# Two-layer transformer kernel: the order of scores, divisions, rotary work and layer norm in the attention stages of its first attention layer

## The chip, the core and the metric

The kernel runs on one core of a Trainium2 chip. Its engines are TensorE (PE in the profile, with weight loads as PEld), VectorE (DVE), ScalarE (ACT), GpSimd (POOL) and SyncE (SP, which here only issues DMAs). Each engine works through its own queue in order. The metric is the device time of one execution in microseconds. Three runs before the change took 939.63, 939.76 and 940.93 us; the median is 939.76.

## The reference

The input is x of shape (8, 512, 256) in float32. All matmuls but the quantised one are float32. There are two layers, each x + attention(norm(x)) + feed-forward(norm(x)).

```python
xn = _layernorm(x)
# layer 0 (the code's first attention): 16 heads of 64, rotary positions, causal softmax
q = rope(xn @ Wq + bq); k = rope(xn @ Wk + bk); v = xn @ Wv + bv
attn = softmax(where(causal, q @ k.T / 8, -1e9))
x = x + (attn @ v) @ Wo + bo + quantised_linear(xn)
xn = _layernorm(x)
# layer 1: a gated comparison as attention, and a mix over time as feed-forward
c = (xn @ left) @ (xn @ right).T / 16
x = x + ((c > threshold) * softmax(c + bias)) @ xn + time_mix(xn)
```

The rotary step multiplies each pair of halves by cosines and sines and adds: h = l * cos + swapped(l) * sin. The change touches the first attention alone (the one with 16 heads).

## The kernel before, in words

The first attention is cut into 16 stages, numbered `at` 0 to 15: 8 sequences by 2 groups of 8 heads. The order of instructions on every engine is that of the program text (`manual_schedule`); nothing is rearranged. Inside a stage the work is this.

- **Projections.** `project_qk` (matmuls at L400) makes the queries (`which` 0) or keys (`which` 1) of four heads: 8 matmul records into two PSUM banks, which ScalarE moves to a tile `l` with the bias (L405). Four DMAs on SP's queue copy `l` with its halves exchanged into `y`. `turn_qk` is the rotary step: two products on VectorE (L417, one for `h`, one for `y`), and their sum on GpSimd (L432). `l` and `y` have two buffers each. `project_v` (L443) makes the values, in two halves of two banks; ScalarE copies them out (L449), they go to DRAM, and `load_v` brings them back in the layout that the weighting needs.
- **Scores.** The 16 blocks of 32 query rows, called i, are causal: block i has 32(i+1) columns. `UNITS` packs them into nine units of two PSUM banks each, (15), (14, 0), (13, 1) and so on to (8, 6) and (7). `RUNS` groups the units: runs 0 to 3 have two units each, run 4 has unit (7) alone. `scores(at, run)` is TensorE's part (L480).
- **Softmax.** `soften(at, run)` reads each bank once on VectorE (L508: mask, minimum of the negated scores, and the copy to a tile `p`), which frees the bank, and takes the exponential with its sum on ScalarE (L512). `divide` takes reciprocals on VectorE (L523) and divides on GpSimd (L531), or, with `on_act`, on ScalarE (L529) for the last unit of the run. `turn` transposes 32x32 blocks on VectorE (L551) into the tiles `t0` to `t3`. The `p` tiles have four buffers, so unit 11 takes the buffer of unit 15 once that has been transposed.
- **Weighting and output.** `weigh(at)` (L568) multiplies the values with the transposed chances into four banks; `keep_weighed` moves them out on ScalarE (L582). `output_product` (L362) applies Wo, `add_output` adds on VectorE (L371).
- **Layer norm of later sequences.** `look_at` takes the statistics on VectorE, `prepare` applies them (L171) and takes the greatest magnitude (L301); `transpose_x` turns the result on TensorE (L318). In stages 12 and 13 some work of the quantised layer joins: `round_input` on GpSimd (L190), `clip` on VectorE (L196, L197).

PSUM has one pool of eight banks:

```python
ps = ctx.enter_context(tc.tile_pool(name="ps", bufs=8, space=PSUM))
```

Banks are handed out in turn: a new bank is the one that was handed out eight banks earlier, and the first matmul into it waits until that one's reader has finished. In stage `at` of the kernel before, TensorE's order is: run 0 of the scores (4 banks), the weighting of stage at-1 (4), run 1 (4), the queries of stage at+1 (4), run 2 (4), the values of stage at+1 (4), in even stages the transposes of the next sequence (2), runs 3 and 4 (6), the output product of stage at-1 (2), the keys of stage at+2 (4). Stage 15 and what follows it are written out by hand.

## Time and profile before

| | |
|---|---|
| median of three runs | 939.76 us |
| profiled execution | 939.1 us |
| its span, first to last instruction | 937.2 us |
| granted clock of TensorE | 0.999 |
| TensorE busy | 923.8 us (99%) |
| VectorE busy | 787.4 us (84%) |
| GpSimd busy | 540.0 us (58%) |
| ScalarE busy | 533.0 us (57%) |

Busy times are of the engines' own instructions; issuing DMAs and waiting on semaphores doesn't count. A line of a timeline gives the start and the length in us, engine, source line, operation, the tiles as output<-input, their shapes, and how many instructions were merged into the line; a bracket at its end gives the idle time before it and what ended it. Lengths of neighbouring lines overlap a little, so sums go from start to start. The slices cut the span into 40 equal parts, each digit the busy share in tenths.

### The profile page before, as it was taken

The page shows a single profiled execution, that of the slowest core. Times are in us where ns is not written, and L with a number is a line of the kernel's source. Part 1 is how long each engine was busy: PE and PEld are TensorE (multiplying, and loading weights), DVE is VectorE, ACT ScalarE, POOL GpSimd, SP SyncE. Part 2 cuts the span into 40 slices and gives each one's busy share as a digit, 9 for nine tenths or more (in the row PEclk, how much of TensorE's full clock was granted, in tenths as well). Part 3 has the DMA queues.
Part 4 walks back from the last instruction along what each step waited for, and adds up shares of the span by engine and source line. Part 5 has one row for each costly group of instructions (what it writes and reads, how often), then busy time and mean ns, then how long its engine had stood idle before and what let it go on. Part 6 is the DMA issues. An engine that isn't in the chain of part 4 may idle for free.

```text
span 937.2 us, 27414 instructions
## 1 busy us (share of the span) xinstructions
PE 923.8 (99%) x10491; PEld 600.8 (64%) x10491; DVE 787.4 (84%) x2431; ACT 533.0 (57%) x1488; POOL 540.0 (58%) x688
## 2 busy tenths in 40 slices
PE   9998999999999999999999999999999999999998
PEld 5446565656666575757565656666657777777776
DVE  4998889898799889978997899899899588888854
ACT  3585555656575656474747566555667434445553
POOL 2676765655665757566665756678666424444311
PEclk9999999999999999999999999999999999999999
DMA  7667453525443545263535435453444132211011
GB/s 212 193 166 201 112 128 126 122 80 138 146 105 96 133 136 131 75 159 92 136 91 160 108 98 137 136 145 106 103 114 126 47 101 79 76 57 39 23 34 34
DMA packets 60930, 105.40 MB, mean 112 GB/s; under 512 B 7552, under 2 KB 38272, under 8 KB 60800
## 3 DMA queue, kind: packets, MB, share of 16 engines
q1 hardware_dynamic: 58928, 102.01, 40.1%
q10 hardware_dynamic: 1872, 1.64, 0.7%
q8 instruction: 83, 1.36, 0.6%
q14 instruction: 47, 0.39, 0.1%
HBM read 39.14 MB, written 28.84 MB: 73 GB/s over the span
## 4 chain that ended last, share of the span: by engine, by line
PE 92%; DVE 4%; issue 1%; ACT 1%; POOL 1%; SPq 0%; DMA 0%; DVEq 0%; ACTq 0%; POOLq 0%
PE pq L400 22%; PE av L568 14%; PE sc L480 13%; PE pw L362 12%; PE pv L443 10%; PE po L727 5%; PE pg L689 3%; PE pvv L701 3%; PE pk L674 3%; PE trc L714 1%; PE plr L240 1%; PE c L646 1%; DVE t L551 1%; PE acc L205 1%; DVE p L508 1%
## 5 line engine op out<-in xcount | busy, mean ns | idle before, releaser
L512 ACT ACTIVATE p<-p,nm 128x64 f32<-128x64 f32 (+15 forms) x512 | 259.9, 512 | 123.1 <-DVE nm L508 98.3
L531 POOL TENSOR_SCALAR p<-p,rs 128x512 f32<-128x512 f32 (+4 forms) x504 | 263.3, 543 | 44.0 <-DVE rs L523 41.9
L432 POOL TENSOR_TENSOR h<-h,y 128x1024 f32<-128x1024 f32 x62 | 161.0, 2596 | 188.9 <-DVE y L417 106.6
L508 DVE CUSTOM_DVE_ANT_0 p<-sc,cmask 128x64 f32<-128x64 f32 (+15 forms) x512 | 190.3, 434 | 61.5 <-PE sc L480 61.5
L551 DVE STREAM_TRANSPOSE t<-p 128x256 f32<-128x256 f32 (+3 forms) x640 | 192.1, 366 | 18.2 <-POOL p L531 18.1
L480 PE MATMUL sc<-h,h 64*32 64x416 f32 (+15 forms) x4096 | 138.7, 393 | 1.9 <-POOL h L432 1.2
L568 PE MATMUL av<-t,vr 32*64 32x192 f32 (+15 forms) x4096 | 128.8, 392 | 4.0 <-issue 4.0
L568 PEld LDWEIGHTS av<-t,vr 32*64 32x64 f32 x4096 | 123.2, 131 | 9.1 <-issue 7.8
L480 PEld LDWEIGHTS sc<-h,h 64*32 64x32 f32 x4096 | 78.8, 106 | 76.0 <-issue 56.5
L405 ACT ACTIVATE l<-pq,cs 128x512 f32<-128x512 f32 x128 | 84.7, 683 | 66.8 <-PE pq L400 54.4
L417 DVE TENSOR_TENSOR y<-y,cs 128x1024 f32<-128x1024 f32 x64 | 110.7, 1729 | 5.8 <-DMA y<-l 5.3
L362 PE MATMUL pw<-wo,att 128*128 128x256 f32 x512 | 114.8, 382 | 0.0
L400 PE MATMUL pq<-xnT,wq 128*128 128x512 f32 x256 | 114.6, 599 | 0.2 <-ACT xnT L321 0.2
L443 PE MATMUL pv<-wv,xnT 128*128 128x512 f32 x256 | 114.3, 599 | 0.0
L400 PE MATMUL pq<-xnT,wk 128*128 128x512 f32 x256 | 112.9, 593 | 0.6 <-DVE nm L508 0.6
L362 PEld LDWEIGHTS pw<-wo,att 128*128 128x128 f32 x512 | 95.9, 190 | 18.5 <-issue 6.1
L512 ACT ACTIVATION_READ_ACCUMULATOR p<-p,nm 128x1 f32 x512 | 97.3, 190 | 0.0
L400 PEld LDWEIGHTS pq<-xnT,wk 128*128 128x128 f32 x256 | 48.6, 190 | 56.6 <-issue 54.1
L443 PEld LDWEIGHTS pv<-wv,xnT 128*128 128x128 f32 x256 | 47.3, 190 | 57.9 <-issue 54.1
L417 DVE TENSOR_TENSOR h<-l,cs 128x1024 f32<-128x1024 f32 x64 | 79.5, 1243 | 4.5 <-ACT l L405 4.5
L400 PEld LDWEIGHTS pq<-xnT,wq 128*128 128x128 f32 x256 | 47.2, 190 | 56.0 <-issue 48.8
L582 ACT ACTIVATE att<-av,cs 128x512 f32<-128x512 f32 x64 | 38.7, 688 | 71.4 <-PE av L568 71.4
(113 smaller groups left out, 949.8 us busy)
## 6 DMA issues: line engine op xcount, KB each, us to landing
y<-l SPq DMA_DIRECT2D x256, 128.0 KB, 2.3
va<-v SPq DMA_DIRECT2D x32, 512.0 KB, 3.1
vr<-va SPq DMA_DIRECT2D x64, 256.0 KB, 4.8
x<-in_x SPq DMA_DIRECT2D x15, 512.0 KB, 4.2
xnf<-xnT SPq DMA_DIRECT2D x8, 512.0 KB, 3.3
x1f<-x SPq DMA_DIRECT2D x7, 512.0 KB, 2.7
out<-y SPq DMA_DIRECT2D x14, 256.0 KB, 2.2
cut_wo<-xnf SPq DMA_DIRECT2D x5, 512.0 KB, 4.2
```

Source lines behind the costliest of these rows:

```text
L362: nc.tensor.matmul(pw[:, j, :], atts[at, p][:, tok], wo[:, 4 * (at % NH) + p, :], start=(p == 0), stop=(p == 3),)
L400: nc.tensor.matmul(pb, w[:, g, k, bass.ts(t, P)], xnT[b][:, k, :], start=(k == 0), stop=(k == NK - 1),)
L405: nc.scalar.activation(l[:, t, :], pb, AF.Identity, bias=cs[:, bias : bias + 1])
L417: nc.vector.tensor_tensor(dst, src, table[:, None, :].to_broadcast([P, 2, S]), ALU.mult)
L432: (engine or nc.gpsimd).tensor_tensor(h, h, y, ALU.add)
L443: nc.tensor.matmul(pb.rearrange("p (g n) -> p g n", g=2), xnT[b][:, k, bass.ts(2 * half + j, P)], wqkv[2][:, 2 * g : 2 * g + 2, k, :], sta ...
L480: nc.tensor.matmul(scored[at, i][e][j * Q : j * Q + Q, :], q[rows, j % 2, bass.ts(i, Q)], k[rows, j % 2, :n], start=True, stop=True,)
L508: nc.vector.tensor_tensor_reduce(p[:, e, col : col + n], sc, cmask[:, S - n :], -1.0 / L**0.5, BIG, ALU.add, ALU.min, nm[:, c : c + 1],)
L512: nc.scalar.activation(p[:, e, col : col + n], p[:, e, col : col + n], AF.Exp, bias=nm[:, c : c + 1], scale=-1.0, accum_out=sm[:, c : c + 1],)
L531: nc.gpsimd.tensor_scalar(p, p, rs[:, c : c + 1], 1.0, ALU.mult, ALU.mult)
L551: nc.vector.transpose(turned[at][c][:, :, at_ : at_ + (n - 1) * pitch(c) + 1 : pitch(c), :], p[:, :, c * P : c * P + n * Q].rearrange("p e ...
L568: nc.tensor.matmul(banks[j][e * L : e * L + L, i * Q :], vs[at][rows, m, c, bass.ts(e, L)], t[c][rows, e, m * pitch(c) + m : m * pitch(c) ...
```

## The change

Stage 1 is written out as it was (with its last transposes of `turn(1, 4)` at its end, where they stood at the start of stage 2). In stages 2 to 14 the order changes:

- The scores come in two stretches: runs 0 and 1 together after the weighting, and runs 2, 3 and 4 together between the two halves of the values.
- The weighting of stage at-1 opens the stage. Beside it stand the rotary step of the second queries of this stage (`turn_qk(2 * at + 1, 0)`, which was in the stage before), the statistics of a later sequence and, in most even stages, its layer norm.
- On GpSimd the sum of the second queries, which stood between the divisions of runs 2 and 3, is gone from there, so that the divisions of runs 2, 3 and 4 follow each other. The divisions of run 0 keep their place ahead of the sum of the second keys, and those of run 1 ahead of the sum of the first queries; what moves is VectorE's part: the eviction of run 1 now comes before run 0's reciprocals and products, and that of run 2 only after both rotary steps and both transposes.
- The divisions of unit (8, 6) go from GpSimd to ScalarE (`on_act`).
- Run 4 is transposed at the end of its own stage. `turn` can now take one unit of a run (`part`).

In the hand-written part, run 2 of stage 14 moves there from the loop. The number of instructions is the same on TensorE, VectorE and SP's DMA issues; ScalarE gets 48 divisions that GpSimd had.

```diff
@@ -536,14 +536,14 @@
         def pitch(c):
             return NT * 4 - 4 * c - 1
 
-        def turn(at, run):
+        def turn(at, run, part=slice(None)):
 
             if at not in turned:
                 turned[at] = [
                     prob.tile([P, 2, 4 * pitch(c) + 1, Q], F32, tag=f"t{c}", name=f"t_{at}_{c}", bufs=1)
                     for c in range(NT)
                 ]
-            for i in (i for us in RUNS[run] for i in us):
+            for i in (i for us in RUNS[run][part] for i in us):
                 p = chances.pop((at, i))
                 for c in range(i // 4 + 1):
                     n = min(4, i + 1 - 4 * c)
@@ -810,87 +810,127 @@
         x_next.append(load_x(2))
         turn(0, 3)
         project(2, 1)
-        for at in range(1, last):
+
+        at = 1
+        scores(1, 0)
+        turn(0, 4)
+        soften(1, 0)
+        weigh(0)
+        keep_weighed(0)
+        load_rest()
+        load_second()
+        fetch(0)
+        turn_qk(4, 1)
+        load_v(1)
+        divide(1, 0)
+        turn_qk(5, 1)
+        scores(1, 1)
+        soften(1, 1)
+        turn(1, 0)
+        divide(1, 1)
+        project(2, 0)
+        scores(1, 2)
+        soften(1, 2)
+        turn_qk(4, 0)
+        turn(1, 1)
+        divide(1, 2)
+        nc.gpsimd.tensor_tensor(bob, bob, rw[:, 2, :], ALU.add)
+        add_biases(0)
+        project_v(2)
+        scores(1, 3)
+        soften(1, 3)
+        turn_qk(5, 0)
+        turn(1, 2)
+        divide(1, 3)
+        scores(1, 4)
+        soften(1, 4)
+        finish(0)
+        turn(1, 3)
+        project(3, 1)
+        divide(1, 4)
+        turn(1, 4)
+        for at in range(2, last):
             b, g = divmod(at, NH)
             two = at + 2 <= last
+            clips = at in (last - 3, last - 2)
             if g == 0 and b < B - 1:
                 fetch(b)
-            scores(at, 0)
-            turn(at - 1, 4)
-            soften(at, 0)
             if at == last - 3:
                 scale_of_x()
             weigh(at - 1)
+            if at > 2:
+                turn_qk(2 * at + 1, 0)
+            if at == 2 or g == 1 and 1 <= b < B - 2:
+                look_at(b + 1 + g)
+            turn_qk(2 * at + 2, 1)
+            if g == 0 and 1 < b < B - 2:
+                prepare(b + 1)
             keep_weighed(at - 1)
-            if at == 1:
-                load_rest()
-                load_second()
-                fetch(0)
-            turn_qk(2 * at + 2, 1)
             load_v(at)
-            if at in (last - 3, last - 2):
+            if clips:
                 s_ = at - last + 3
                 fetch_output(s_, output_tile(f"x1e_{s_}"))
                 xnl = fetch_input(s_, work.tile([P, NK, S], F32, tag="xnl", name=f"xnl_{s_}"))
+            if at == last - 2:
+                first_norm = norm(0, xpool.tile([P, NT, D], F32, tag="x", name="yn_0"))
+            scores(at, 0)
+            scores(at, 1)
+            soften(at, 0)
+            project_qk(2 * at + 2, 0)
+            soften(at, 1)
             divide(at, 0)
             turn_qk(2 * at + 3, 1)
-            if at == last - 2:
-                first_norm = norm(0, xpool.tile([P, NT, D], F32, tag="x", name="yn_0"))
-            scores(at, 1)
-            soften(at, 1)
-            turn(at, 0)
             if at == 2:
-                look_at(2)
+                prepare(2)
             elif at == 4:
                 spread_rest()
                 spread_second()
-            elif g == 1 and 1 <= b < B - 2:
-                look_at(b + 2)
+            elif at == last - 1:
+                first_norm()
+            project_qk(2 * at + 3, 0)
+            if clips:
+                round_input(xnl)
+            turn(at, 0)
             divide(at, 1)
-            if at == last - 1:
-                first_norm()
-            project(at + 1, 0)
-            if at in (last - 3, last - 2):
-                round_input(xnl)
-            scores(at, 2)
-            soften(at, 2)
             turn_qk(2 * at + 2, 0)
             turn(at, 1)
-            if at in (last - 3, last - 2):
+            if at == last - 4:
+                prepare(b + 2)
+            if clips:
                 xq = work.tile([P, NK, S], BF16, tag="xq", name=f"xq_{s_}")
                 clip(xnl, xq)
-            divide(at, 2)
-            if at == 2:
-                prepare(2)
-            elif g == 1 and 1 <= b < B - 2:
-                prepare(b + 2)
             if at == last - 1:
                 turn_qk(2 * at + 3, 0)
-            if at == 1:
-                nc.gpsimd.tensor_tensor(bob, bob, rw[:, 2, :], ALU.add)
-                add_biases(0)
-            project_v(at + 1)
-            if at == last - 1:
+                project_v(at + 1)
                 break
+            project_v(at + 1, (0,))
+            for run in (2, 3, 4):
+                scores(at, run)
+            soften(at, 2)
+            soften(at, 3)
+            project_v(at + 1, (1,))
             if g == 0 and b < B - 1:
                 transpose_x(b + 1)
                 if b + 2 < B:
                     x_next.append(load_x(b + 2))
-            scores(at, 3)
-            soften(at, 3)
-            turn_qk(2 * at + 3, 0)
-            turn(at, 2)
-            divide(at, 3)
-            scores(at, 4)
+            divide(at, 2)
+            turn(at, 2, slice(0, 1))
+            divide(at, 3, on_act=True)
+            turn(at, 2, slice(1, 2))
             soften(at, 4)
-            if at in (last - 3, last - 2):
+            if clips:
                 for half in range(2):
                     add_quantised(s_, half, xq, line(f"u_{s_}_{half}"))
-            finish(at - 1)
-            turn(at, 3)
+            for half in range(2):
+                output_product(at - 1, half)
+            turn(at, 3, slice(0, 1))
+            divide(at, 4)
+            turn(at, 3, slice(1, 2))
+            for half in range(2):
+                add_output(at - 1, half)
+            turn(at, 4)
             if two:
                 project(at + 2, 1)
-            divide(at, 4)
             if g == 0 and b < B - 1:
                 add_biases(b)
             if at == last - 4:
@@ -898,9 +938,11 @@
 
 
         at = last
-        scores(at - 1, 3)
-        soften(at - 1, 3)
+        for run in (2, 3):
+            scores(at - 1, run)
+            soften(at - 1, run)
         nc.sync.dma_start(w2, second.rearrange("j (k p) n -> p j k n", p=P))
+        divide(at - 1, 2)
         turn(at - 1, 2)
         divide(at - 1, 3)
         scores(at - 1, 4)
```

## The prediction

> **What bounds the kernel now.** I read the page's busy shares and slices first, then TensorE's timeline for one stage, then its waits, then the timelines of VectorE and GpSimd over the same stretch.

> ```profile
> PE 923.8 (99%) x10491; PEld 600.8 (64%) x10491; DVE 787.4 (84%) x2431; ACT 533.0 (57%) x1488; POOL 540.0 (58%) x688
> PE   9998999999999999999999999999999999999998
> DVE  4998889898799889978997899899899588888854
> PEclk9999999999999999999999999999999999999999
> ```

> TensorE has work all the time, at the full granted clock; VectorE is second. The profiled execution took 939.1 us, 0.7 below the median of 939.76, with a span of 937.2. TensorE idles 13.4 us in all, so no order of the same matmuls can gain more than that.

> TensorE's timeline, one stage (stage 5):

> ```profile
> 254.71 1.95 PE L480 MATMUL sc<-h,h 64*32 64x512 f32 x48
> 256.59 8.02 PE L568 MATMUL av<-t,vr 32*64 32x512 f32 x256
> 264.54 2.12 PE L480 MATMUL sc<-h,h 64*32 64x448 f32 x64
> 266.58 7.13 PE L400 MATMUL pq<-xnT,wq 128*128 128x512 f32 x16
> 273.65 2.01 PE L480 MATMUL sc<-h,h 64*32 64x384 f32 x64
> 275.59 7.13 PE L443 MATMUL pv<-wv,xnT 128*128 128x512 f32 x16
> 282.65 2.39 PE L480 MATMUL sc<-h,h 64*32 64x320 f32 x80
> 284.97 7.17 PE L362 MATMUL pw<-wo,att 128*128 128x256 f32 x32
> 291.98 7.03 PE L400 MATMUL pq<-xnT,wk 128*128 128x512 f32 x16
> 298.94 1.95 PE L480 MATMUL sc<-h,h 64*32 64x512 f32 x48
> ```

> Start to start the pieces take: run 0 of the scores 1.88, weighting 7.95, run 1 2.05, queries 7.06, run 2 1.94, values 7.06, runs 3 and 4 2.32, output 7.01, keys 6.96; 44.23 in all, without a gap. Between any two groups of score banks lie some 7 us of other matmuls: the time VectorE has to empty the banks.

> TensorE's waits in stages 2 to 13 come to 3.2 us (line L480 adds 1.2 in stage 14).

> VectorE (rotary products L417) and GpSimd (rotary sums L432, divisions L531), from their timelines around 305 and 103 us:

> ```profile
> 303.96 1.22 DVE L417 TENSOR_TENSOR y<-y,cs 128x1024 f32<-128x1024 f32 x1
> 305.25 1.20 DVE L417 TENSOR_TENSOR h<-l,cs 128x1024 f32<-128x1024 f32 x1
> 306.36 3.38 DVE L417 TENSOR_TENSOR y<-y,cs 128x1024 f32<-128x1024 f32 x1
> ...
> 305.32 3.34 POOL L432 TENSOR_TENSOR h<-h,y 128x1024 f32<-128x1024 f32 x1 [5.80 <-DVE rs L523]
> 312.74 2.37 POOL L432 TENSOR_TENSOR h<-h,y 128x1024 f32<-128x1024 f32 x1
> ...
> 101.29 5.67 POOL L531 TENSOR_SCALAR p<-p,rs 128x384 f32<-128x384 f32 x8 [0.46 <-DVE rs L523]
> 237.76 3.65 POOL L531 TENSOR_SCALAR p<-p,rs 128x384 f32<-128x384 f32 x8 [0.47 <-DVE rs L523]
> ```

> A product that meets a sum takes 3.38 instead of 1.22 and ends when the sum has ended and 1.1 us more have passed; the sum takes 3.34 instead of 2.37. The eight divisions that met two products at 103.9 to 106.4 took 5.67 instead of 3.65. So a product and a GpSimd instruction take turns. Transposes and the scores' eviction show no such loss beside divisions.

> **The change, part by part.** TensorE's matmuls are the same ones. What changes is how much of them lies between a bank's filling and its next use. In stages 2 to 13 the new order is weighting, runs 0 and 1 (eight banks at one go), queries, half the values, runs 2, 3, 4 (ten banks), the other half of the values, output, keys. The eight PSUM banks go round, so run 4 takes the banks of unit 11, the first of run 2, and waits in TensorE's queue until VectorE has evicted it (L508). Behind that wait stands everything else of TensorE. And VectorE now does two rounds of rotary products and both transposes of runs 0 and 1 ahead of that eviction.

> I take time 0 as the start of the eviction of unit 15, 0.22 after its matmuls end (317.88+0.97 to 319.07 in the trace). TensorE then needs: unit 14, 0.94; run 1, 2.05; queries 7.06; half the values 3.5; run 2, 1.94; run 3, 0.8 of 2.32 = 1.86; less 0.22. It wants run 4's bank at 17.1.

> VectorE and GpSimd, each step as soon as its engine and its input are there:
> - eviction of runs 0 and 1: 2.58 + 2.76 (rows at 300.25 and 309.98) = 5.34; reciprocals to 5.5. ScalarE's exponentials of run 0 start at about 1.4, behind the four weighted banks (2.42), take 3.4 and are in time.
> - two products (key, second half), 1.14 each start to start: to 7.8. GpSimd's divisions of run 0 meet them and take turns; unit 15's two divisions (0.65 each) end at 9.1, the rest of run 0 (1.3 + 0.6) at 11.0.
> - transposes of run 0 from 9.1: 2.7, to 11.8; reciprocals to 12.0.
> - GpSimd's rotary sum 11.0 to 13.4. VectorE's next two products (the first queries) want to start at 12.0, wait to 13.4, end at 15.65.
> - only then run 1's divisions: 3.65, to 19.3; transposes follow, ending at 20.0.
> - eviction of unit 11: 1.38, to 21.4.

> TensorE stands from 17.1 to 21.5: 4.4. Run 4 takes 0.47 to 22.0; the second half of the values wants unit 10's banks, free at 22.6: 0.6 more. **5.0 us per stage.** From there: values 3.5, output 7.0, keys 6.96 to 40.1. VectorE and its suppliers: eviction of runs 2 and 3 to 25.5; exponentials of run 3, 3.95 on ScalarE, to 28.6; transposes of unit 10 to 30.4; run 4's eviction 31.1; ScalarE's four divisions (rows 534 and 474 ns) about 2 us, then run 4's exponentials to 33.8; its divisions 35.0; transposes of unit 8, two output additions (1.2) and run 4's transposes to 37.6. The weighting, which now has no run 0 ahead as cover (1.88), finds its input 2.5 us early.

> The other parts:
> - The second queries' rotary work moves beside the weighting: four products and two sums, taking turns, some 6.5 us, plus 3.3 for a layer norm in the even stages, with 9.1 us and the 2.5 in hand: no cost. If that cover were gone, scores of run 0 would wait for the sum.
> - The four exchange copies per projection stay in SP's order. The keys' last copy waits for the second queries' sum, now a stage later, with the next load of values queued behind it; the copy lands in 2.3, the load in 4.8, and both are wanted tens of us later: nothing.
> - Fewer changes of tile shape on TensorE: run 2's 1.94 against run 1's 2.05 bounds this at 0.1 gained or lost per stage, taken at nothing.
> - Stage 2: weighting without cover costs 1.9 more (it already waited 0.86 at 118.84). Its layer norm (3.2) falls where VectorE waits for GpSimd anyway: 0.6.
> - Stage 11: layer norm of the last sequence ahead of run 2's eviction, four of 0.5 and one of 1.22: 3.15.
> - Stages 12 and 13: rounding on GpSimd (1.12) ahead of run 1's divisions and clipping (1.1) ahead of run 2: 2.2 each, 4.4.
> - Stage 14: 3.5 us more of values on TensorE, against two more products held up by a sum: wait 4.8.
> - Old gaps that close as TensorE is late: 2.7.

> Sum: 12 x 5.0 + 1.9 + 0.6 + 3.15 + 4.4 + 4.8 - 2.7 = 72. From 939.1 that is 1011; with the 0.7 to the median, **1012**.

> A rule on the clock, weighed: the trace's clock stays at 1.00 in its windows through its longest gap, 2.31 us (L568, at 72.6), and no row shows a longer one once the work has begun. [...] I keep the full clock, as the nearest rows show it.

> **The rivals.**
> - Products and GpSimd don't take turns there, or find free places. Then unit 15's divisions end at 6.9, run 0's transposes at 10.6, products at 13.1, run 1's transposes at about 16, unit 11 at 17.4: 0.3 + 0.6 per stage. 12 x 0.9 + 1.9 + 0.6 + 3.15 + 4.4 + 1.5 - 2.7 = 20, so 959. Against it: 5.67 for 3.65, 3.38 for 1.22. Chance 0.12.
> - Not slower: VectorE reaches unit 11's eviction by 17.1 in each stage. That decides it; it needs 4.3 us less between 0 and 21.4, when VectorE's own instructions there add up to 17.3 without any wait. Then the 4.4 of gaps in stages 2 to 14 go: 935 to 941. Only evictions much shorter than the rows would give it. Chance 0.05.
> - The end of the stage is late too: ScalarE carries four more divisions and the values' evictions ahead of run 4's exponentials. Up to 2.5 us later costs nothing; beyond that every us costs 12. At 4.5 late: 24, 1036. Against it: ScalarE was 57% busy. Chance 0.08.
> - The clock falls after each wait: if the 3.5 us of values that follow took half as long again, 13 x 1.75 = 23, 1035. For it: waits longer than any shown; against: clock 1.00 so far. Chance 0.08.

> **How the numbers follow.** My own case has 0.67, and its own range is 980 to 1025: a wait of 2.5 to 6 per stage. The range that should hold the time 8 times in 10 reaches down into the case without turns and up to the two late ones: 958 to 1034. A change of under 0.2% (1.9 us) can't be told from none. Faster 0.03, same 0.02 (both from the second rival), slower 0.95.

> **What would show it.** Among TensorE's waits a new row for L480, released by VectorE's nm L508, about 12 to 13 times, 4 to 5 us each; a smaller one of L443 behind it. Stages of 49 us. VectorE's products before run 0's and run 1's transposes lengthened, and VectorE waiting for L531. No wait of L568 beyond stage 2. Wrong would be: run 4 following run 3 without a gap, or the wait at another line; a lower granted clock would point to the last rival.

## The result and the profile after

| | before | after |
|---|---|---|
| median, us | 940.35 (939.63 to 941.96, 4 runs) | 1034.47 (1034.33 to 1036.46, 4 runs) |
| span of the profiled execution, us | 937.2 | 1034.6 |
| TensorE busy, us | 923.8 | 955.1 |
| TensorE idle, us | 13.4 | 79.5 |
| mean granted clock of TensorE | 0.999 | 0.949 |

The change makes the kernel 10% slower: the ratio is 1.1007, with a 95% interval of 1.0989 to 1.1024. The prediction was 1012, with a range of 958 to 1034. Of the 97.4 us between the two spans, 66.1 are idle time of TensorE and 31.3 are the same 10491 matmul records taking longer. Idle time was forecast (72); the longer matmuls were a rival's (23).

From the page of the kernel after, the busy times, and the slices of TensorE, VectorE and the granted clock:

```profile
PE 955.1 (92%) x10491; PEld 610.6 (59%) x10491; DVE 808.3 (78%) x2431; ACT 547.1 (53%) x1536; POOL 544.6 (53%) x640
...
PE   9989979898989898989898969698897999999998
...
DVE  4997696889687868786888696787869948888864
...
PEclk9999999999989898989898989899898999999999
```

From the twelfth slice to the 26th every second digit of TensorE falls, and the clock's digit falls with it in each of them. All in all the clock says that some 105 us (0.051 of 1034.6, doubled since it falls to a half, 0.50 in the window from 306 to 308 below) were spent at half clock.

TensorE's waits, largest first (line, releaser; us in total, times, longest):

```profile
PE sc L480 <- DVE nm L508: 66.6, 13, 9.8
PE av L568 <- issue: 4.9, 2, 2.6
```

One wait, 13 times, at the line and by the releaser that the prediction named. TensorE's timeline for stage 5, which answers to the one shown of before:

```profile
276.77 7.88 PE L568 MATMUL av<-t,vr 32*64 32x512 f32 x256
284.58 3.98 PE L480 MATMUL sc<-h,h 64*32 64x512 f32 x112
288.49 7.13 PE L400 MATMUL pq<-xnT,wq 128*128 128x512 f32 x16
295.46 3.60 PE L443 MATMUL pv<-wv,xnT 128*128 128x512 f32 x8
298.99 3.74 PE L480 MATMUL sc<-h,h 64*32 64x384 f32 x128
306.68 1.31 PE L480 MATMUL sc<-h,h 64*32 64x256 f32 x16 [3.96 <-DVE nm L508]
308.02 5.53 PE L443 MATMUL pv<-wv,xnT 128*128 128x512 f32 x8
313.40 7.07 PE L362 MATMUL pw<-wo,att 128*128 128x256 f32 x32
320.30 7.03 PE L400 MATMUL pq<-xnT,wk 128*128 128x512 f32 x16
```

The next weighting starts at 327.26, so the stage takes 50.49 where it took 44.23. Start to start, the piece from run 2 to the end of run 4 takes 9.03 (298.99 to 308.02) against 1.94 + 2.32 = 4.26: 4.77 more. The values take 3.53 + 5.38 against 7.06: 1.85 more. All else together is 0.36 less. The two halves of the values have the same shape and count; the half ahead of the wait takes 3.60, the half behind it 5.53.

The clock over that stretch, by windows (busy time and count of TensorE, weight loads, VectorE, ScalarE and GpSimd, then the granted clock, DMA share, GB/s):

```profile
302.00:304.00 2.00, 0.73 (x32) 0.26 (x12) 1.58 (x6) 0.00 (x0) 2.00 (x6) 1.00 0.47 132
304.00:306.00 2.00, 0.00 (x0) 0.00 (x0) 2.00 (x8) 0.06 (x1) 2.00 (x3) 0.74 0.54 188
306.00:308.00 2.00, 1.31 (x16) 0.43 (x17) 2.00 (x13) 2.00 (x9) 0.83 (x1) 0.50 0.00 0
308.00:314.00 6.00, 5.98 (x11) 2.92 (x12) 4.56 (x26) 6.00 (x26) 2.93 (x7) 0.68 0.00 0
314.00:320.00 6.00, 6.00 (x29) 5.28 (x29) 5.61 (x22) 3.46 (x10) 3.46 (x8) 1.00 0.28 90
```

0.74 over two us means half clock for 1.04 of them, so it fell at 304.96, in the midst of the gap; 0.68 over six means half clock for 3.84, so it came back at 311.8. In between lie run 4 and most of the second half of the values.

VectorE and GpSimd in the same stage, with lines left out; time 0 of the prediction, the start of unit 15's eviction, is 285.76:

```profile
292.38 1.22 DVE L417 TENSOR_TENSOR y<-y,cs 128x1024 f32<-128x1024 f32 x1
294.78 2.79 DVE L551 STREAM_TRANSPOSE t<-p 128x256 f32<-128x256 f32 x9 [1.18 <-POOL p L531]
...
297.61 2.35 DVE L417 TENSOR_TENSOR h<-l,cs 128x1024 f32<-128x1024 f32 x1
299.87 1.21 DVE L417 TENSOR_TENSOR y<-y,cs 128x1024 f32<-128x1024 f32 x1
302.16 1.49 DVE L551 STREAM_TRANSPOSE t<-p 128x256 f32<-128x256 f32 x5 [1.07 <-POOL p L531]
303.90 1.48 DVE L551 STREAM_TRANSPOSE t<-p 128x256 f32<-128x256 f32 x5 [0.26 <-POOL p L531]
305.31 0.52 DVE L508 CUSTOM_DVE_ANT_0 p<-sc,cmask 128x384 f32<-128x384 f32 x1
```

```profile
291.38 5.18 POOL L531 TENSOR_SCALAR p<-p,rs 128x512 f32<-128x512 f32 x6 [9.27 <-DVE rs L523]
296.52 2.35 POOL L432 TENSOR_TENSOR h<-h,y 128x1024 f32<-128x1024 f32 x1
298.85 5.66 POOL L531 TENSOR_SCALAR p<-p,rs 128x448 f32<-128x448 f32 x8
```

VectorE's product of 297.61 lasts 2.35 instead of 1.2 because GpSimd's sum runs from 296.52 to 298.87; the eight divisions behind it take 5.66 instead of 3.65 because they share the time with that product's second half and the next one. VectorE waits 1.18, 1.07 and 0.26 for divisions. That is the chain that holds unit 11's eviction (305.31) back.

In the last stages the same wait is longer. TensorE in stages 11 to 13, then what VectorE waited for in stage 12:

```profile
617.44 1.32 PE L480 MATMUL sc<-h,h 64*32 64x256 f32 x16 [7.77 <-DVE nm L508]
...
673.80 1.31 PE L480 MATMUL sc<-h,h 64*32 64x256 f32 x16 [9.79 <-DVE nm L508]
...
728.99 1.31 PE L480 MATMUL sc<-h,h 64*32 64x256 f32 x16 [7.51 <-DVE nm L508]
```

```profile
664.63 1.65 DVE L417 TENSOR_TENSOR y<-y,cs 128x1024 f32<-128x1024 f32 x1 [3.40 <-DMA y<-l]
```

The exchange copy of the queries comes 3.40 us late. In these two stages the whole normalised input is fetched on the same queue ahead of it. In stage 13 VectorE doesn't wait for that copy, but the first part of the clipping takes 2.06 us there, as it does in stage 12, against 0.66 in the kernel before:

```profile
725.17 2.06 DVE L196 TENSOR_SCALAR xq<-xnl 128x1024 bf16<-128x1024 f32 x1
```

### The profile page after: what moved, and what is told of

The parts are those of the page before. It is cut to its first block, busy times and chain, and to the rows that moved or that the text cites. A ratio compares the mean times of both kernels' runs of the same rounds, so it can differ in the third digit from the quotient of the medians.

```text
span 1034.6 us, 27351 instructions
## 1 busy us (share of the span) xinstructions
PE 955.1 (92%) x10491; PEld 610.6 (59%) x10491; DVE 808.3 (78%) x2431; ACT 547.1 (53%) x1536; POOL 544.6 (53%) x640
## 4 chain that ended last, share of the span: by engine, by line
PE 63%; DVE 14%; POOL 11%; issue 5%; DMA 3%; ACT 2%; SPq 1%; DVEq 0%; POOLq 0%; ACTq 0%
PE av L568 12%; PE pq L400 11%; PE pw L362 9%; POOL p L531 9%; DVE p L508 7%; PE pv L443 7%; PE po L727 5%; PE sc L480 4%; PE pk L674 3%; PE pg L689 3%; PE pvv L701 3%; DVE t L551 2%; DMA y<-l 2%; POOL h L432 2%; PE c L646 1%
## 5 line engine op out<-in xcount | busy, mean ns | idle before, releaser
L531 POOL TENSOR_SCALAR p<-p,rs 128x512 f32<-128x512 f32 (+6 forms) x456 | 272.6, 618 | 208.1 <-DVE rs L523 207.7
L508 DVE CUSTOM_DVE_ANT_0 p<-sc,cmask 128x64 f32<-128x64 f32 (+15 forms) x512 | 188.1, 434 | 56.4 <-PE sc L480 56.3
L432 POOL TENSOR_TENSOR h<-h,y 128x1024 f32<-128x1024 f32 x62 | 148.9, 2402 | 124.0 <-DVE y L417 113.0
L480 PE MATMUL sc<-h,h 64*32 64x32 f32 (+15 forms) x4096 | 143.6, 405 | 67.1 <-DVE nm L508 66.6
L480 PEld LDWEIGHTS sc<-h,h 64*32 64x32 f32 x4096 | 86.6, 108 | 122.6 <-issue 109.7
L443 PE MATMUL pv<-wv,xnT 128*128 128x512 f32 x256 | 139.4, 697 | 0.4
L568 PE MATMUL av<-t,vr 32*64 32x224 f32 (+15 forms) x4096 | 130.5, 400 | 5.7 <-issue 4.9
L568 PEld LDWEIGHTS av<-t,vr 32*64 32x64 f32 x4096 | 114.0, 133 | 30.7 <-issue 24.5
L362 PE MATMUL pw<-wo,att 128*128 128x256 f32 x512 | 115.6, 384 | 0.1
L400 PE MATMUL pq<-xnT,wq 128*128 128x512 f32 x256 | 114.6, 599 | 0.2 <-ACT xnT L321 0.2
L400 PE MATMUL pq<-xnT,wk 128*128 128x512 f32 x256 | 112.9, 592 | 0.6 <-DVE nm L508 0.6
L417 DVE TENSOR_TENSOR h<-l,cs 128x1024 f32<-128x1024 f32 x64 | 103.2, 1613 | 7.9 <-ACT l L405 7.9
L362 PEld LDWEIGHTS pw<-wo,att 128*128 128x128 f32 x512 | 97.6, 192 | 18.1 <-issue 4.8
L417 DVE TENSOR_TENSOR y<-y,cs 128x1024 f32<-128x1024 f32 x64 | 85.0, 1328 | 25.1 <-DMA y<-l 24.4
L443 PEld LDWEIGHTS pv<-wv,xnT 128*128 128x128 f32 x256 | 56.7, 228 | 79.9 <-issue 68.7
L400 PEld LDWEIGHTS pq<-xnT,wk 128*128 128x128 f32 x256 | 48.6, 190 | 56.6 <-issue 52.4
L400 PEld LDWEIGHTS pq<-xnT,wq 128*128 128x128 f32 x256 | 47.2, 190 | 56.0 <-issue 49.5
```

Source lines behind the costliest of these rows:

```text
L362: nc.tensor.matmul(pw[:, j, :], atts[at, p][:, tok], wo[:, 4 * (at % NH) + p, :], start=(p == 0), stop=(p == 3),)
L400: nc.tensor.matmul(pb, w[:, g, k, bass.ts(t, P)], xnT[b][:, k, :], start=(k == 0), stop=(k == NK - 1),)
L417: nc.vector.tensor_tensor(dst, src, table[:, None, :].to_broadcast([P, 2, S]), ALU.mult)
L432: (engine or nc.gpsimd).tensor_tensor(h, h, y, ALU.add)
L443: nc.tensor.matmul(pb.rearrange("p (g n) -> p g n", g=2), xnT[b][:, k, bass.ts(2 * half + j, P)], wqkv[2][:, 2 * g : 2 * g + 2, k, :], sta ...
L480: nc.tensor.matmul(scored[at, i][e][j * Q : j * Q + Q, :], q[rows, j % 2, bass.ts(i, Q)], k[rows, j % 2, :n], start=True, stop=True,)
```

## The experiments

Two theories stood against each other. The first: the loss beyond the forecast is the half clock that follows each gap, so it goes if TensorE is kept busy through the gap. The second: it is something else that slows the values behind the gap (their banks come free late, or ScalarE's copies hold them), and then filling the gap changes nothing. A second set of runs asks which of the change's moves makes the gap. In each of these kernels everything else is as in the kernel after, unless the text says otherwise.

**Work in the gap.** In stages 2 to 13, one to four matmuls of a constant (some 0.9 us each, 3.70 for four) go into unit 8's own pair of banks, which run 4 doesn't need, ahead of unit 8's scores, which overwrite them. They compute nothing that is used.

```diff
+                if fill and us == RUNS[3][0]:
+                    spare[at] = [bank(f"sc_{at}_{RUNS[3][1][0]}_{e}") for e in range(2)]
+                    for m in range(fill):
+                        nc.tensor.matmul(spare[at][m % 2], ident, cs[:, :S], start=True, stop=True)
...
-            for run in (2, 3, 4):
-                scores(at, run)
+            scores(at, 2)
+            scores(at, 3, FILL)
+            scores(at, 4)
```

> Four extra matmuls (128x512, about 3.5 us) ahead of unit 8's scores, written to unit 8's own bank and overwritten, so that in the usual stages TensorE's idle time before run 4 falls from 3.96 us to about 0.5 and nothing else moves. Theory, the clock: TensorE's clock halves after an idle time of 3.9 us and more, and that makes run 4 (1.31 us) and the second half of the values (5.5 to 6.0 us) slow. Then run 4 goes back to about 0.66, the values to 3.5, the usual stage from 50.5 to about 49.2 (odd) and from 51.9 to 50.3 (even), and the time to about 1019 (1013 to 1023), the three stages with longer waits keeping their slow values. Rival: the values are slow because of the banks or of what VectorE and ScalarE read meanwhile; then they stay at 5.5 and the time at 1034, or more by what the extra matmuls cost.

> Two extra matmuls ahead of unit 8 instead of four: about 1.75 us of work, so the usual stage's idle time before run 4 falls from 3.96 to about 2.2 us, while run 4 starts when it did. Theory, the clock: an idle time of 2.2 us doesn't lower it, so run 4 and the values are as fast as with four extra matmuls and the time is the same, about 1016 (1012 to 1020). Rival: the four extra matmuls helped by work that lies closer to run 4 or by the banks; then two help about half, 1025.

> One extra matmul: about 0.87 us, leaving an idle time of about 3.1 us in nine usual stages. The runs so far show an idle time of 3.05 us with the clock kept (e2_evict_early) and 3.44 and 3.53 with the clock lowered (e2_evict_early, e3_no_product). If the bound lies between, nearly all nine stages keep the clock: 1016 to 1021. If idle times of a little over 3 us lower it now and then, some stages show slow values: 1021 to 1031. Rival: any idle time of 3 us lowers it: 1034.

> Three extra matmuls, leaving about 1.0 us idle before run 4 in the usual stages (and 0.47 behind it). With two extra the idle times were 1.88 and 0.47 and the clock fell in eight of nine usual stages; with four they were 0.17 and 0.47 and it fell in none. If the clock goes by the share of idle time in its 3.4 us steps, 1.5 us of idle time should leave it full in most stages: about 1016 to 1020. Rival: what lowers it is the single short run 4 between two waits, whatever their length; then it falls here as with two: 1028.

| matmuls added | time, us | ratio to before (95%) | clock | usual gap ahead of run 4 | values behind it |
|---|---|---|---|---|---|
| 0 (the kernel after) | 1034.47 | 1.1007 (1.0989 to 1.1024) | 0.949 | 3.96 | 5.53 |
| 1 | 1028.20 | 1.0944 (1.0918 to 1.0969) | 0.972 | 2.74 | 5.37, in two stages 3.67 |
| 2 | 1028.64 | 1.0937 (1.0909 to 1.0965) | 0.972 | 1.88 | 5.37, in one stage 3.67 |
| 3 | 1013.71 | 1.0787 (1.0758 to 1.0816) | 0.988 | 1.02 | 3.67 |
| 4 | 1015.63 | 1.0798 (1.0771 to 1.0825) | 0.988 | 0.17 | 3.67 |

TensorE with three and with two matmuls added, at the end of the wait:

```profile
299.80 0.87 PE L486 MATMUL sc<-h,h 64*32 64x256 f32 x16 [1.02 <-DVE nm L518]
301.14 3.67 PE L444 MATMUL pv<-wv,xnT 128*128 128x512 f32 x8 [0.47 <-DVE nm L518]
```

```profile
306.24 0.87 PE L486 MATMUL sc<-h,h 64*32 64x256 f32 x16 [1.88 <-DVE nm L518]
307.59 5.37 PE L444 MATMUL pv<-wv,xnT 128*128 128x512 f32 x8 [0.47 <-DVE nm L518]
```

More work on TensorE makes the kernel 20.8 us shorter (three matmuls: 1034.47 to 1013.71), and the values behind the gap go back to 3.67 in each of the eight usual stages (3 to 10). VectorE's order and ScalarE's copies are those of the kernel after, and the values wait 0.47 for a bank in both of these runs. So the slow values were the clock, and the second theory falls. The run with two matmuls missed what was expected of it: I had taken the clock to hold once the gap was under the 2.31 us of the trace before, and at 1.88 + 0.47 us, with only run 4's 0.87 between, it fell in seven of the eight usual stages. With one the time lay in the expectation's second case (1021 to 1031), though the gap was 2.74 and not the 3.1 that it spoke of; with three it came out 2 us below its range. The 3.4 us that the last expectation names is the length of a low stretch in the run with two matmuls: 0.76 + 2.00 + 0.64, by the clock of 0.81, 0.50 and 0.92 in its windows from 204 to 206, 206 to 208 and 208 to 212.

**Which move makes the gap.** First, run 2's eviction goes ahead of run 1's transposes (half the values and the scores go with it), and so, in stages 11 to 13, also ahead of the layer norm and the clipping:

```diff
             turn_qk(2 * at + 2, 0)
+            if at < last - 1:
+                project_v(at + 1, (0,))
+                for run in (2, 3, 4):
+                    scores(at, run)
+                soften(at, 2)
             turn(at, 1)
...
-            project_v(at + 1, (0,))
-            for run in (2, 3, 4):
-                scores(at, run)
-            soften(at, 2)
             soften(at, 3)
```

> Only the place of run 2's eviction changes: on VectorE it comes ahead of run 1's transposes instead of behind them (ScalarE's exponentials with it). Theory, the place in VectorE's queue: run 4 no longer waits; the wait that is next is for unit 9's banks at the sequence transposes or the output product, about 1 us per stage, under which the clock stays full; with the later stages' extra waits the time is about 970 (950 to 985). Rival: ten banks in one stretch out of eight are too many whatever VectorE's order; then run 4 still waits about 4 us and the time stays over 1020.

Second, the second stretch alone is undone: run 2 stands between the halves of the values, runs 3 and 4 behind them.

```diff
             project_v(at + 1, (0,))
-            for run in (2, 3, 4):
-                scores(at, run)
+            scores(at, 2)
             soften(at, 2)
-            soften(at, 3)
             project_v(at + 1, (1,))
...
+            for run in (3, 4):
+                scores(at, run)
+            soften(at, 3)
             divide(at, 2)
```

> The second stretch alone is undone: run 2 between the halves of the values, runs 3 and 4 after the second half (and after the sequence transposes), as before; run 3's eviction follows as before the divisions. All else is the changed kernel. Theory, the second stretch asks for run 2's banks too early: TensorE has 3.5 us more to do first, so about 1 to 1.5 us of wait is left at run 3, too short to drop the clock; with the later stages' extra waits 965 to 980. Rival: the first stretch or the weighting at the head of the stage is what costs; then the time stays over 1010.

Third, both together:

```diff
             turn_qk(2 * at + 2, 0)
+            if at < last - 1:
+                project_v(at + 1, (0,))
+                scores(at, 2)
+                soften(at, 2)
             turn(at, 1)
...
+            for run in (3, 4):
+                scores(at, run)
+            soften(at, 3)
             divide(at, 2)
```

> The second stretch undone as in e4_split, and run 2's eviction ahead of run 1's transposes as in e2_evict_early. What stays of the change in the usual stages is the first stretch, the weighting at the head with the second queries' rotary work beside it, and the four divisions on ScalarE. Theory: these cost nothing by themselves; no wait of the scores in the usual stages, a usual stage of 44.3 to 45, and a time of 958 to 970, which is what stages 2 and 11 to 14 still lose. Rival: the first stretch or the work beside the weighting costs 1 us or more per stage; then 972 or more.

| | run 2 evicted behind both transposes | run 2 evicted ahead of run 1's transposes |
|---|---|---|
| runs 2, 3, 4 in one stretch | 1034.47 (the kernel after) | 971.76, ratio 1.0336 (1.0321 to 1.0352) |
| runs 3, 4 behind the values | 998.42, ratio 1.0617 (1.0596 to 1.0639) | 951.15, ratio 1.0111 (1.0089 to 1.0133) |

The early eviction came out as expected, the undone stretch 18 us above its range, the two together 7 below theirs. The undone stretch by itself still lets the clock fall in the even stages (64 matmuls of runs 3 and 4 in 3.54 us, where all 80 took 2.39 in the kernel before):

```profile
345.56 3.54 PE L480 MATMUL sc<-h,h 64*32 64x320 f32 x64 [1.90 <-DVE nm L508]
```

The kernel with both, one odd stage of TensorE:

```profile
263.84 3.98 PE L480 MATMUL sc<-h,h 64*32 64x512 f32 x112
...
278.25 2.01 PE L480 MATMUL sc<-h,h 64*32 64x384 f32 x64
280.19 3.70 PE L443 MATMUL pv<-wv,xnT 128*128 128x512 f32 x8
283.82 2.39 PE L480 MATMUL sc<-h,h 64*32 64x320 f32 x80
...
307.92 2.54 PE L480 MATMUL sc<-h,h 64*32 64x512 f32 x56
```

No wait, and 44.08 from stage to stage, where the kernel before takes 44.23. From the weighting of stage 2 (118.20) to that of stage 12 (569.56) it takes 451.4, against 451.7 in the kernel before (118.84 to 570.57). So the first stretch, the weighting at the head of the stage, the second queries' rotary step beside it and the four divisions on ScalarE together cost nothing there. The loss is the place of one eviction (62.7 us with the second stretch, 47.3 without) and the second stretch (36.0 with the late eviction, 20.6 with the early one). What remains lies at the end: of the 12.3 us between the two spans (949.5 and 937.2), 10.9 lie between the weighting of stage 12 and that of stage 15 (144.75 against 133.81).

**The second stretch by itself,** in the order of the kernel before (stages 2 to 13, one half of the values ahead, runs 2, 3 and 4 in a row):

```diff
-            scores(at, 2)
+            joined = 1 < at < last - 1
+            if joined:
+                project_v(at + 1, (0,))
+            for run in (2, 3, 4) if joined else (2,):
+                scores(at, run)
             soften(at, 2)
...
-            project_v(at + 1)
+            project_v(at + 1, (1,) if joined else (0, 1))
```

> The kernel before with the second stretch alone: in stages 2 to 13 runs 2, 3 and 4 stand between the halves of the values, all else in its old order, so that VectorE evicts run 2 at once, ahead of the products and of run 1's transposes, and run 3 behind them. Theory: run 4's bank comes in time, and what is late is run 3's: the sequence transposes or the output product want unit 9's banks some 2.5 us too early; about 2.5 to 3 us per stage, 965 to 985. Rival: the second stretch costs nothing if run 2 is evicted at once, because VectorE has idle time: 938 to 950.

976.01, ratio 1.0379 (1.0363 to 1.0395): as expected. It pays at one place that the theory named, the sequence transposes, and at one that it didn't, the weighting:

```profile
248.81 0.66 PE L318 MATMUL pxt<-ident,x 128*128 128x128 f32 x4 [2.08 <-DVE nm L508]
...
311.99 9.70 PE L568 MATMUL av<-t,vr 32*64 32x512 f32 x256 [2.95 <-issue]
```

The even stages wait at the transposes of the next sequence, and the weighting behind an odd stage waits for its input and then takes 9.70 for 8.05, close to the 9.58 and 9.77 of the kernel after behind the gaps of 2.32 and 2.57 at which the clock fell.

**The turn-taking.** The four products that stand in the chain become transposes of the same tiles, which have one input. (This kernel leaves out the products of the second keys and of the first queries in stages 2 to 14, so its scores are of other data.)

```diff
-            turn_qk(2 * at + 3, 1)
+            turn_qk(2 * at + 3, 1, True)
...
-            turn_qk(2 * at + 2, 0)
+            turn_qk(2 * at + 2, 0, True)
```

> In the two rotary steps between the evictions of run 1 and run 2, VectorE's four products are replaced by transposes of the same elements (four of 0.28 us for one product of 1.14), so the queries and keys of these steps are not rotated and the output is another. VectorE has the same work but nothing that takes turns with GpSimd. Theory, the turns: run 0's divisions end some 2.3 us and run 1's some 4 us sooner, run 4's wait falls from 3.96 to about 0.5 in the usual stages, the clock stays full there, the time is 960 to 975. Rival: VectorE's own work is the delay; the wait stays near 4 us and the time over 1020.

```profile
293.85 0.87 PE L486 MATMUL sc<-h,h 64*32 64x256 f32 x16 [0.97 <-DVE nm L514]
295.19 3.67 PE L449 MATMUL pv<-wv,xnT 128*128 128x512 f32 x8 [0.47 <-DVE nm L514]
```

984.60, ratio 1.0460 (1.0433 to 1.0488). The usual wait fell from 3.96 to 0.97, and VectorE no longer waits for a division in the usual chain. The four transposes that stand in for one product take 1.31 together, start to start, where a free product takes 1.14; over the four products that is 0.7 of the 0.97; without turns the wait would be about 0.3, which is what the walk gave for that case. The time is 10 above the range: stages 2 and 11 to 14 still waited 3.5 to 6.8 each, where I had expected them to shrink as the others did.

**The late stages.** Stage 11's layer norm goes behind run 3's eviction. In stages 12 and 13 the large fetches go behind the queries' exchange copies, the rounding behind run 2's divisions, and the clipping and the quantised product to the end of the stage.

```diff
             soften(at, 3)
+            if at == last - 4:
+                prepare(b + 2)
             project_v(at + 1, (1,))
...
             divide(at, 2)
+            if clips:
+                round_input(xnl)
             turn(at, 2, slice(0, 1))
...
                 project(at + 2, 1)
+            if clips:
+                xq = work.tile([P, NK, S], BF16, tag="xq", name=f"xq_{s_}")
+                clip(xnl, xq)
```

> The changed kernel, with the extra work of stages 11 to 13 taken out of the chain ahead of run 2's eviction: stage 11's layer norm behind run 3's eviction, stages 12 and 13's fetches behind the queries' exchange copies, rounding behind run 2's divisions, clipping and the quantised product at the stage's end. Theory: the waits of 7.77, 9.79 and 7.51 us before run 4 in these stages fall to about 4, the time to about 1021 (1017 to 1027). Rival: what makes these stages wait longer is something else (the granted clock, the output additions); then they stay over 7 us and the time at 1034.

1026.37, ratio 1.0928 (1.0908 to 1.0948). The waits at run 4 of stages 11 to 13 fell to 3.96, 3.96 and 3.95, 13.2 us in all, but the time only by 8.1; 5 came back, most of it at the start of stage 13's scores. TensorE in stage 13:

```profile
699.31 3.91 PE L480 MATMUL sc<-h,h 64*32 64x512 f32 x104 [3.31 <-POOL h L432]
...
721.34 1.31 PE L480 MATMUL sc<-h,h 64*32 64x256 f32 x16 [3.95 <-DVE nm L508]
```

**Two attempts at a faster kernel.** The first takes the early eviction with the one stretch, puts the first queries' products behind run 3's eviction, and moves the late stages' work as above. The second starts from the kernel of 951.15 and puts run 0 of stage 2 ahead of the weighting again, stage 14's run 2 ahead of its transposes, the transpose of the scale behind the weighting and the quantised product behind the output product.

```diff
+            if at == 2:
+                scores(at, 0)
             weigh(at - 1)
...
-            turn_qk(2 * at + 2, 0)
...
             divide(at, 2)
+            turn_qk(2 * at + 2, 0)
```

> All of it together: run 2's eviction ahead of run 1's transposes, the first queries' products behind run 3's eviction, the late stages' extra work out of the way as in e5_late, stage 14 in the same order, run 0 of stage 2 ahead of the weighting as cover. The two stretches, the weighting at the head and the four divisions on ScalarE stay. Theory, the changed kernel loses by VectorE's order alone: no wait of run 4 in the usual stages, the clock full, the usual stage 44.2 to 45, the time 938 to 950. Rival: the two stretches themselves cost 1 us or more per stage wherever the eviction stands; then over 955.

```diff
+            if at == 2:
+                scores(at, 0)
+            weigh(at - 1)
             if at == last - 3:
                 scale_of_x()
-            weigh(at - 1)
...
-            if at < last - 1:
-                project_v(at + 1, (0,))
-                scores(at, 2)
-                soften(at, 2)
+            project_v(at + 1, (0,) if at < last - 1 else (0, 1))
+            scores(at, 2)
+            soften(at, 2)
```

> The run with the evictions of run 2 ahead and the second stretch undone (951.15) waits no longer in its usual stages, so what is left of its 11 us over the kernel before lies in stages 2 and 11 to 15: 4.4 us at run 4 of stage 14 with an output product at low clock behind it (5.00 for 3.5, 1.5), 1.5 at the transpose of the scale, 0.6 and 2.1 at the quantised product, 1 to 2 at stage 2's weighting. This kernel does five things to these. In stage 14 the second half of the values and run 2 with its eviction go ahead of the transposes of run 1 and of the second queries' rotary step, as in the other stages; in stage 2 run 0 goes ahead of the weighting again as its cover; the transpose of the scale goes behind the weighting; the quantised product goes behind the output product. My theory, that the whole loss is waits of TensorE for evictions and inputs that lie late in a queue and low clock after them, says that 9 to 13 of the 11 go and the time is 938 to 943, level with the kernel before, with run 4 of stage 14 waiting under 1 us. The rival, that each wait taken away only moves to the next late input (VectorE has no room left in these stages), says 947 or more, with new waits of the same sum at other lines of the same stages.

The first took 977.06 (1.0403, 1.0385 to 1.0421), the second 957.17 (1.0188, 1.0170 to 1.0205). Both missed; the time of the first lies where its rival had it, and of the second the rival was right. The first has no wait at run 4 in its usual stages, but stages 3 and 4 together take 91.46 us (weighting to weighting, 162.24 to 253.70) against 89.52 in the kernel before, with a new wait of 1.20 at the weighting that opens the even stages; from stage 12 on it waits 4.36 at the transpose of the scale, 3.65 at a quantised product and 4.60 at the scores. Of the second, stage 2 ended 2 us earlier, and the 4.44 at run 4 of stage 14 was gone (1.49 came back at run 0 of stage 15), but TensorE met these instead:

```profile
581.22 6.53 PE L480 MATMUL sc<-h,h 64*32 64x512 f32 x104 [4.92 <-POOL h L432]
...
719.94 9.88 PE L568 MATMUL av<-t,vr 32*64 32x512 f32 x256 [2.54 <-DVE t L551]
```

The wait of 4.92 is of my making. On VectorE the scale's reduction (L339) waits for its transpose on TensorE, which now came at 574.53, and the four rotary products queue behind it: they started at 575.49, and with them the sum of the second queries, for which the scores wait, was late. No kernel of these runs beats the one before.

## Why the prediction was wrong

**The step that failed** is the choice on the clock: "I keep the full clock, as the nearest rows show it". The nearest row was a single gap of 2.31 us, and it was made to speak for a gap of 4.4. That the row showed the full clock was itself luck: the same gap, at the same instruction, lost the clock in the kernel after (last section). The clock did fall in each of the 13 waits. Behind the usual wait the values took 1.85 us longer; the rival that was given 0.08 had 1.75 per stage, 23 in all, and 1035. That rival's term, added to my own sum, gives 1035, and 1034.47 was measured. That close a match is partly luck: the idle time came out 6 us below the sum (66.1 for 72) and the longer matmuls 8 above the rival's term (31.3 for 23); 1.5 of these 31.3 lie at stage 1's weighting (9.58 for 8.05), which the change leaves alone. The gap forecast was almost twice the longest one that the trace held, so no row bounded the term at nothing; it belonged in the sum.

The length of the gap would have been no sure sign either: gaps of 3.96 us lowered the clock, but 1.88 + 0.47 us lowered it too, in seven of eight stages, and a single 3.05 (the output product of stage 11 with the early eviction, which took 7.14) did not.

**What held.**

| step, us from the start of unit 15's eviction | predicted | measured |
|---|---|---|
| run 0's transposes start | 9.1 | 9.0 |
| second two products end | 15.65 | 15.3 |
| unit 11's eviction starts | 20.0 | 19.6 |
| TensorE wants run 4's bank | 17.1 | 17.0 |
| run 4 starts | 21.5 | 20.9 |
| run 2 to run 4, over before, per stage | 5.0 | 4.77 |

The wait itself was 3.96 for 4.4. The 0.6 ahead of the values did not show as a wait, since run 4 at half clock took 1.31 and hid it; at full clock, in the filled runs, it is the 0.47 there. The mechanism, the turns of products with sums and divisions, is shown by the run without the products.

**Terms that were off.** Stages 12 and 13 were priced at 2.2 each for rounding and clipping; their waits lie 5.83 and 3.55 above the usual 3.96. In both the clipping took 2.43 (725.17 to 727.60 in stage 13) where 1.1 was priced; why it is longer than in the kernel before isn't shown. The rest of stage 12's is a DMA: VectorE waited 3.40 for an exchange copy. SP's queue carries 512 KB fetches ahead of it, which I counted nowhere; that they delay it is argued from the order alone, and in stage 13, with fetches ahead too, that copy cost no wait. Stage 11's 3.15 measured 3.81, stage 14's 4.8 measured 4.45. Stage 2's weighting without its cover idled 2.57, against 0.86 + 1.9 = 2.8 predicted, but that gap too lowered the clock, and the weighting took 9.77 for 7.87; its run 4 waited 1.5 more than usual, for 0.6. So the errors went both ways: twelve waits of the usual length make 47.5 us of idle time (12 x 3.96) where 60 were forecast, the rest 18.6 (66.1 - 47.5) where 12 were. Run 4's own lengthening at half clock, which filled the 0.6, is counted among the 31.3.

**The other rivals.** Without turns (959): excluded by the lines above; the run that removes them by force also shows what it would be worth. Not slower: VectorE started unit 11's eviction 2.6 us after TensorE had come to want its bank. A late end of the stage (1036): no; the weighting behind the usual stage has no wait.

## What to carry to other kernels

Ask of each PSUM bank in rotation who must have read it before its next use, and what stands ahead of that read in the reader's in-order queue: here one eviction stood behind 4.2 us of transposes and waits in the usual stage (301.08 to 305.31), and moving it alone took back 62.7 of the 94 us lost. A gap on TensorE had a second price here, the low clock after it (31.3 us of longer matmuls beside 66.1 of idle time), and such a price belongs in the sum even when the gap forecast is a short one (1.88 + 0.47 us lowered the clock in seven of eight stages): a row with the full clock behind such a gap shows one case, not a rule. Moves that cost nothing in the usual stage can still be lost in the odd ones at the end, where other queues are full; price those stages one by one, their DMAs too.

## What was new about the hardware

```profile
72.57 8.05 PE L568 MATMUL av<-t,vr 32*64 32x512 f32 x256 [2.31 <-issue]
```

```profile
72.87 9.58 PE L568 MATMUL av<-t,vr 32*64 32x512 f32 x256 [2.32 <-issue]
```

In these traces what differs is how the gap lies in the steps. In the kernel after, one step held almost all of it, and TensorE was busy for 1.12 of that step's 3.41 us; in the kernel of 951.15 two steps shared the same gap. By steps, the kernel after and then that of 951.15:

```profile
69.43:72.85 3.42, 1.12 (x40) 0.47 (x25) 3.25 (x12) 1.33 (x3) 1.84 (x5) 1.00 0.90 281
72.85:76.26 3.41, 3.39 (x34) 2.64 (x42) 3.41 (x14) 2.48 (x7) 0.00 (x0) 0.50 0.67 155
```

```profile
67.40:70.82 3.42, 2.72 (x50) 0.80 (x49) 2.81 (x11) 2.92 (x6) 3.42 (x7) 1.00 0.93 281
70.82:74.23 3.41, 1.80 (x36) 1.83 (x43) 3.41 (x12) 0.89 (x3) 0.01 (x1) 1.00 0.92 237
```

Counted over the trace of the kernel after from 20 to 930 us: of the 236 steps at full clock, 15 had TensorE busy for less than 0.36 of their length, and each was followed by a step at half clock; the other 221 had 0.77 or more, and none was. Of the 31 at half clock, the 15 with 0.93 or more busy were followed by full clock, and the 16 with less than 0.77 were not. In the kernel before, with its steps reckoned back from its one change, at 935.82, the step with most of that gap (68.84 to 72.25) was busy for 1.42 us, 0.42 of its length, and full clock followed. These shares were read from traces made for other questions; no run was made to test them.
- **More work, less time.** Three useless matmuls per stage, 34 us of TensorE's time in all (2.84 in each of 12 stages), made the kernel 20.8 us faster, since they ran inside a gap: in stage 5 1.02 + 0.47 us of it were left of 3.96, and the values behind it took 3.67 instead of 5.53.
